# Four layers with mixtures of experts on one core: indirect transfers of layer 1's second list and of layer 2 in groups of four, each behind the last landing

## The chip, the cores and the metric

The kernel runs on one core of a Trainium2 chip. The metric is device time in microseconds (us), lower is better. Before the change the median of three runs is 2391.09 us (2387.86 to 2400.4). A core has a matrix engine (TensorE, PE in the profile), two engines for elementwise work (VectorE, DVE; ScalarE, ACT), a general engine that issues the indirect transfers here (GpSimd, POOL), and an engine that issues ordinary transfers (SyncE, SP). They run side by side, each through its own list of instructions in order, and wait for each other by semaphores.

## The reference

The input is 4 sequences of 1024 tokens with 128 features, float32. Eight sublayers follow, each of the form "normalise (x + f(x))":

```
x = norm(x + L0_attn(x))   gated scan over time        x = norm(x + L0_ffn(x))  a quantised linear layer
x = norm(x + L1_attn(x))   complex diagonal recurrence x = norm(x + L1_ffn(x))  16 experts, top 4, and a shared one
x = norm(x + L2_attn(x))   causal softmax, 16 heads    x = norm(x + L2_ffn(x))  8 low-rank experts, top 2
x = norm(x + L3_attn(x))   Toeplitz mix, 8 heads       x = norm(x + L3_ffn(x))  32 experts, top 4, and a shared one
```

In the three mixtures a token's result is a weighted sum over its few chosen experts. The reference applies every expert to every token and weights by zero where it was not chosen:

```python
combine = (one_hot(topk_idx, E) * tw[..., None]).sum(1)
h = einsum('td,edf->etf', x, gate_w);  u = einsum('td,edf->etf', x, up_w)
y = einsum('etf,efd->etd', silu(h) * u, down_w)
routed = einsum('etd,te->td', y, combine)
```

## The kernel before

The kernel computes an expert only for the tokens that chose it. The 4096 tokens are 32 tiles of 128, held on the chip in `self.x`. For each mixture and each part of the tokens, a routing step (`l1_route`, `l2_route`, `l3_route`, which end in `positions`) works out, for every token and each of its k choices, a row number in a list that is sorted by expert. The row numbers stand in a tile named `pos` plus the list's name. Lists are tensors in device memory.

A list is filled by `spread` (L1313): for each tile of 128 tokens and each of the k choices one indirect transfer writes the tile's 128 rows of 512 bytes to the 128 positions. The experts then read the list four tiles at a time through `gathered` (L1328, an SP transfer `xg<-...` that waits for all transfers of the spread), compute, and write their rows to a second list. `collect` (L1381) brings the results back: per tile k indirect transfers into a tile `yt`, and then k DVE operations at L1392 that multiply by the routing weight and add to `x`. All indirect transfers, in both directions, are issued by `indirect` on POOL (L1301). Names in the profile follow: `l1rr<-x,posl1r` is a scatter of layer 1's list r, `yt<-l1yr,posl1r` a gather of its results.

Layer 1 has two lists: a (the first half of the sequences, 64 transfers each way) and r (the second half, 64). Layer 2 has three, from two halves of attention: a2 (32 transfers each way), m2 and n2 (16 each). Layer 3 has a (64), b and c (32 each).

The order of the program is written by Python generators. Each step of a generator emits some instructions and yields their planned time in us. `mix(main, side)` (L238) runs the main generator and, after each of its steps, as many side steps as fit in its planned time; the side's instructions thus fall between those of the main one in each engine's list. `chain` puts generators one behind the other, `abreast` beside each other, `served` starts another one when a condition holds, and `press` runs a side alone until a condition holds. `self.now` is the sum of planned time. `moved_by` is the planned end of the indirect transfers so far; each adds 1.26 us. `collect` emits a tile's additions once `now` has passed its planned end by 4 us, or waits for that when the `yt` buffers (five for l1r, eight for l2a) are all in use.

The stages that matter here, from `all` (L1895), with the time at which each ran in the profiled execution:

- about 620 to 890 us: `l2_attn(0)`, attention of layer 2 for the first half, with the routing and the spread of l1r beside it.
- 890 to 1058 us: the experts of l1r and its shared expert, with the routing and the spread of l2a (`routed(a2)`) beside them.
- 1058 to 1207 us: `l2_experts(a2)`, with `l1_close(r)` beside it, which collects l1r's results, normalises, saves x (`xsave`) and transposes for the next attention.
- 1207 to 1603 us: `l2_attn(1)`, with `rows_in(a2)` (the collection of l2a's results), then `onward(a)`, layer 3's mix, routing and spread for part a, and `routed(m2)` when half of the rows are ready, `routed(n2)` when all are.
- 1603 to 1864 us: `l2_experts(m2)` and `l2_experts(n2)`, with what is left of that side.
- from about 1890 us: layer 3's shared expert and experts, part by part, with spreads and collections between them.

On POOL, the indirect transfers are kept in their order by two order-only dependencies on the last transfers (`self.moved`). They do not wait for each other's landing. Transfers of one spread are declared independent (`apart`), because they write different rows. POOL also reads, ahead of a rarely taken branch, how many tiles a list uses (`rest_of`, L1354).

Of the kernel before, what the change touches and what calls it, by code (L numbers as in the profile page):

```python
# [21 lines left out]
B, L, D = 4, 1024, 128  # L22
# [18 lines left out]
E1, F1, NG1, TKG1, K1 = 16, 128, 4, 2, 4  # L41
# [33 lines left out]
class Kernel:  # L75
    def __init__(self, ctx, tc, ins, out, cols, consts, rows):
        self.tc, self.nc, self.ins, self.out = tc, tc.nc, ins, out
        self.count = itertools.count()
        nc = self.nc
        self.const = self.pool(ctx, "const")  # L80
        self.small = self.pool(ctx, "small", 3)
        self.routes = self.pool(ctx, "routes")
        self.side = self.pool(ctx, "side", 2, space=PSUM)
        dram = self.pool(ctx, "dram", space=DRAM)

        self.cols_t = self.load(self.const, ins["cols"])
        self.cst_t = self.load(self.const, ins["consts"])
        self.x = self.tile(self.const, [P, NT, D], "x")
        self.xT = self.tile(self.const, [P, NT * P], "xT")
        nrow = ins["rows"].shape[1]  # L90
        self.rows_t = self.tile(self.const, [P, nrow], "rows")
        nc.gpsimd.dma_start(out=self.rows_t, in_=ins["rows"].to_broadcast([P, nrow]))
        self.col = {k: self.cols_t[:, a:b] for k, (a, b) in cols.items()}
        self.cst = {k: self.cst_t[:, a:b] for k, (a, b) in consts.items()}
        self.row = {k: self.rows_t[:, a:b] for k, (a, b) in rows.items()}
        self.ident = self.cst["ident"]
        self.eps = self.tile(self.const, [P, 1], "eps")
        nc.vector.memset(self.eps, LN_EPS)
        self.halfpi = self.tile(self.const, [P, 1], "halfpi")
        nc.vector.memset(self.halfpi, math.pi / 2)  # L100
        self.ones = self.tile(self.const, [P, E3], "ones")
        nc.vector.memset(self.ones, 1.0)
        self.rnd = self.tile(self.const, [P, 1], "rnd")
        nc.vector.memset(self.rnd, RND)
        self.zero = self.tile(self.const, [P, D], "zero")
        nc.gpsimd.memset(self.zero, 0.0)
        self.flag = self.tile(self.const, [1, 1], "flag", I32)
        self.hm = self.tile(self.const, [P, 4], "hmg")

        self.first, self.rest = Part("a", 0, 2), (Part("b", 2, 1), Part("c", 3, 1))  # L110
        self.parts = (self.first, *self.rest)
        self.by_rows = (
            Part("a", 0, 2, range(B), 0), Part("m", 2, 2, (0, 1), NT // 2), Part("n", 2, 2, (2, 3), 3 * NT // 4)
        )

        self.rows_done = 0

        self.listed = set()

        self.traced, self.latest = nc.cur_bb.bb.instructions, {}  # L120
        self.now = self.moved_by = 0.0
        self.moved = []

        self.lists, self.route = {}, {}
        self.both = (self.first, Part("r", 2, 2))
        for lay, ne, k in (("l1", E1, K1), ("l2", E2, K2), ("l3", E3, K3)):
            for pt in {"l1": self.both, "l2": self.by_rows, "l3": self.parts}[lay]:
                tl = -(-((pt.nt * P * k + (P - 1) * ne) // P) // 4) * 4
                self.lists[lay, pt.name] = (
                    self.tile(dram, [tl * P, D], f"{lay}r{pt.name}"), self.tile(dram, [tl * P, D], f"{lay}y{pt.name}"), tl  # L130
                )
        self.wall2 = self.tile(dram, [P, E2 * 3 * F2], "wall2")
        self.xsave = self.tile(dram, [P, NT, D], "xsave")

        self.ksave = self.tile(dram, [P, B, BLK], "ksave")
        self.vsave = self.tile(dram, [P, B, 4, (NH + 1) * VW], "vsave")
# [1162 lines left out]
    def indirect(self, apart=(), **kw):  # L1299

        ins = self.nc.gpsimd.indirect_dma_start(**kw)  # L1301

        for o in apart:
            self.tc.declare_no_dep(ins.ins, o.ins.name, reason="rows differ")
        behind = mybir.DependencyInfo(mybir.DependencyClass.NoSync, mybir.DependencyReason.DATA)
        mine = [o.ins.name for o in apart]
        for o in [o for o in self.moved if o not in mine][-2:]:
            self.tc.add_manual_dep(ins.ins, o, behind, reason="queued behind")
        self.moved = self.moved[-130:] + [ins.ins.name]
        self.moved_by = max(self.moved_by, self.now) + 1.26  # L1310
        return ins

    def spread(self, lay, part, k):  # L1313

        pos, _, _, done, _ = self.route[lay + part.name]
        rows = self.lists[lay, part.name][0]
        for t in range(part.nt):
            for i in range(k):
                ins = self.indirect(
                    apart=done,  # L1320
                    out=rows, out_offset=bass.IndirectOffsetOnAxis(ap=pos[:, t, i : i + 1], axis=0),
                    in_=self.x[:, part.order[t], :], in_offset=None,
                )
                done.append(ins)
            yield (1.26 * k,)
        self.listed.add(lay + part.name)

    def gathered(self, pool, rows, g, done, want):  # L1328
# [52 lines left out]
    def collect(self, lay, part, k, yp, first=0, nt=None, which=None):  # L1381

        nc = self.nc
        pos, wk = self.route[lay + part.name][:2]
        assert f"made {lay}{part.name}" in self.listed
        ys = self.lists[lay, part.name][1]
        late = []

        def add():
            t, yt, _ = late.pop(0)  # L1390
            for i in range(k):
                nc.vector.scalar_tensor_tensor(  # L1392
                    self.x[:, part.order[t], :], yt[:, i, :], wk[:, t, i : i + 1], self.x[:, part.order[t], :],
                    ALU.mult, ALU.add,
                )

        for t in which or range(first, first + (nt or part.nt)):
            yt = self.tile(yp, [P, k, D], "yt")
            for i in range(k):
                self.indirect(  # L1400
                    out=yt[:, i, :], out_offset=None, in_=ys,
                    in_offset=bass.IndirectOffsetOnAxis(ap=pos[:, t, i : i + 1], axis=0),
                )

            late.append((t, yt, self.moved_by + 4.0))
            if len(late) == yp.bufs:
                while late[0][2] > self.now:
                    yield (1.0,)
                add()
            yield (1.26 * k,)  # L1410
        while late:
            while late[0][2] > self.now:
                yield (1.0,)
            add()
            yield (0.36 * k,)
# [479 lines left out]
    def all(self):  # L1895
        a, rest = self.first, self.rest
        b, c = rest
        r = self.both[1]
        a2, m2, n2 = self.by_rows
        with ExitStack() as ctx:  # L1900
            lgp = self.pool(ctx, "l2lg")
            self.l2_lg = self.tile(lgp, [P, NT, E2], "lg")
            with ExitStack() as early:
# [13 lines left out]
                with ExitStack() as c2:  # L1917
                    wall = self.l1_wall(c2)
                    yp = self.pool(c2, "l1ya", 5, right=True)
# [2 lines left out]
                    self.run(self.mix(self.abreast(self.l2_weights(), side), self.l1_close(a, yp)))  # L1922
            with ExitStack() as c2:
                wall = self.l1_wall(c2)
                self.run(self.mix(self.l2_attn(0), self.chain(self.l1_route(r), self.spread("l1", r, K1))))
                wall2, loads = self.l2_wall(c2, True)
                yp = self.pool(c2, "l1yr", 5, right=True)
                self.run(self.mix(self.chain(self.l1_experts(r, wall), self.l1_shared(r)), self.chain(loads, self.routed(a2))))
                self.run(self.mix(self.l2_experts(a2, wall2), self.l1_close(r, yp)))
            listed = lambda name: lambda: name in self.listed  # L1930
            on = self.served(
                self.chain(self.rows_in(a2), self.onward(a, True)),
                (lambda: self.rows_done >= B + 2, self.routed(m2)),
                (lambda: self.rows_done == 2 * B, self.routed(n2)),
            )
            self.run(self.mix(self.l2_attn(1), on, drain=False))
            with ExitStack() as c3:
                with ExitStack() as c2:
                    wall = self.l2_wall(c2)
# [7 lines left out]
                yp = self.pool(c3, "l3y", 8)  # L1947
# [23 lines left out]
        with self.tc.If(bad > 0):  # L1971
            with ExitStack() as ctx:
# [9 lines left out]
                for p in self.parts:  # L1982
                    self.run(self.onward(p))
                    with ExitStack() as c2:
                        sw, wall = self.l3_wall(c2)
# [167 lines left out]
```

## Time and profile before

| what | value |
|---|---|
| median of three runs | 2391.09 us |
| profiled execution, its own time | 2410.17 us |
| span in the profile, mean granted TensorE clock | 2408.4 us, 0.828 |
| PE busy | 1599.0 us (66%), 9017 matmuls |
| DVE busy | 1262.4 us (52%) |
| ACT busy | 822.5 us (34%) |
| POOL busy | 720.1 us (30%) |
| indirect transfers, queue q0 | 20704 packets, 42.86 MB, 5.8% of 16 DMA engines |
| l1rr<-x: 64 transfers | 699.1 to 779.9 us, median 958 ns |
| l2ra<-x: 32 transfers | 951.5 to 991.7 us, median 958 ns |
| yt<-l1yr: 64 transfers | 1021.3 to 1180.3 us, median 945 ns |
| yt<-l2ya: 32 transfers | 1210.1 to 1289.8 us, median 944 ns |
| l2rm<-x and l2rn<-x: 16 transfers each | from 1483.9 and from 1647.8 us, median 958 ns |

The time of a transfer in the table is how long POOL is busy with it; between two that follow each other POOL shows 0.30 us more. Busy time counts only work: register, branch, semaphore and transfer-issuing instructions of the other engines are not in it. Idle time of an instruction is put down to a releaser, the instruction of another engine whose signal came last before it started. "Issue" is idle time in which the engine waited for nothing that the profile shows; "remote" is a wait for a signal whose sender the profile can't place as late.

### The profile page before, as it was taken

The numbers are of one execution on the slowest core, as the hardware profiler recorded it, in microseconds if no ns is written. First come the engines' busy times: TensorE is split into PE (matmuls) and PEld (weight loads), VectorE is DVE, ScalarE is ACT, GpSimd is POOL, SyncE is SP. The second block draws the span as 40 slices with busy tenths as digits, with TensorE's granted clock in tenths as the row PEclk, the third lists the DMA queues.
The fourth block names the chain that finished last, engine by engine and source line by source line (L and its number), as shares of the span: only waits on it lengthen the run. The fifth ranks groups of instructions, "written<-read, shape, count | busy, mean of one in ns | idle before, by whom it ended". The sixth has DMA issues, their size and how long they took to land. (4 is left out here: it accounts for less than half of the span.)

```text
span 2408.4 us, 27028 instructions
## 1 busy us (share of the span) xinstructions
PE 1599.0 (66%) x9017; PEld 956.7 (40%) x9017; DVE 1262.4 (52%) x3630; ACT 822.5 (34%) x1179; POOL 720.1 (30%) x681
## 2 busy tenths in 40 slices
PE   7625776975661778487969797887735798357160
PEld 3214334843320347344623232344423486155160
DVE  8857894655570655224535674573602265237133
ACT  6701671422230433122336554632101164233030
POOL 1031483135227001325132002002272200735725
PEclk9866887988785889688979998988877899678575
DMA  9930002334101015212130000031411131222232
GB/s 309 288 112 0 21 34 93 115 115 157 62 30 50 15 54 185 81 42 76 40 101 21 1 1 18 1 119 36 160 71 32 42 113 49 78 81 59 90 88 68
DMA packets 215529, 187.10 MB, mean 78 GB/s; under 512 B 16528, under 2 KB 194064, under 8 KB 214864
## 3 DMA queue, kind: packets, MB, share of 16 engines
q1 hardware_dynamic: 194672, 142.29, 18.7%
q0 software_dynamic: 20704, 42.86, 5.8%
q8 instruction: 84, 1.38, 0.2%
q14 instruction: 69, 0.57, 0.1%
HBM read 88.49 MB, written 96.60 MB: 77 GB/s over the span
## 5 line engine op out<-in xcount | busy, mean ns | idle before, releaser
L1055 ACT ACTIVATE pr<-sc 128x1024 f32<-128x1024 f32 x288 | 279.5, 1021 | 319.3 <-PE sc L157 186.3
L157 PE MATMUL gu<-ld,xgT 128*128 x640 | 176.9, 423 | 75.3 <-ACT xgT L167 57.4
L157 PE MATMUL sc<-qm,kT 32*128 32x512 f32 (+3 forms) x1536 | 200.0, 555 | 14.2 <-ACT pr L1055 7.4
L157 PE MATMUL s<-pr,va 128*32 128x512 f32 (+3 forms) x1536 | 174.0, 520 | 45.9 <-issue 25.9
L1755 DVE TENSOR_TENSOR hg<-sg,gu 128x256 f32<-128x256 f32 x160 | 65.7, 417 | 210.7 <-ACT sg L1754 194.9
L157 PEld LDWEIGHTS gu<-ld,xgT 128*128 128x128 f32 x640 | 127.9, 211 | 104.6 <-ACT xgT L167 60.7
L165 PE MATMUL tp<-ld,hg 128*128 128x128 f32 x624 | 103.5, 288 | 95.2 <-DVE hT L169 44.2
L157 PE MATMUL gu<-wall,xgT 128*128 x304 | 155.0, 636 | 2.7 <-ACT xgT L167 2.0
L169 DVE COPY hT<-tp 128x512 f32<-128x512 f32 x118 | 80.9, 686 | 140.5 <-remote 65.5
L1061 DVE TENSOR_TENSOR pr<-pr,ld 128x512 f32<-128x512 f32 (+1 forms) x160 | 92.2, 580 | 101.0 <-ACT pr L1055 98.5
L165 PE MATMUL tp<-ld,xg 128*128 128x128 f32 x396 | 67.7, 300 | 112.4 <-DMA xg<-l3rc 50.3
L165 PEld LDWEIGHTS tp<-ld,hg 128*128 128x128 f32 x624 | 81.1, 148 | 147.6 <-issue 62.7
L167 ACT COPY xgT<-tp 128x512 f32<-128x512 f32 x99 | 57.8, 585 | 236.9 <-PE tp L165 130.4
L157 PEld LDWEIGHTS sc<-qm,kT 32*128 32x128 f32 x1536 | 85.1, 195 | 116.4 <-issue 76.5
L1507 ACT ACTIVATE sg<-gu 128x512 f32<-128x512 f32 x76 | 45.2, 597 | 215.3 <-PE gu L157 104.9
L1754 ACT ACTIVATE sg<-gu 128x256 f32<-128x256 f32 x160 | 60.9, 384 | 151.5 <-PE gu L157 78.2
L1301 POOL DMA_INDIRECT l1ra<-x,posl1a x64 | 93.0, 1454 | 59.0 <-DVE posl1a L1276 39.8
L157 PEld LDWEIGHTS s<-pr,va 128*32 128x32 f32 x1536 | 38.5, 111 | 153.7 <-issue 106.3
L1301 POOL DMA_INDIRECT yt<-l1yr,posl1r x64 | 60.8, 950 | 127.9 <-DVE x L1392 80.1
L165 PEld LDWEIGHTS tp<-ld,xg 128*128 128x128 f32 x396 | 50.9, 155 | 118.9 <-issue 74.5
L1509 DVE TENSOR_TENSOR hg<-sg,gu 128x512 f32<-128x512 f32 x76 | 51.8, 681 | 80.5 <-ACT sg L1507 57.9
L1301 POOL DMA_INDIRECT l1rr<-x,posl1r x64 | 61.5, 961 | 100.0 <-DVE posl1r L1276 80.8
(440 smaller groups left out, 3471.0 us busy)
## 6 DMA issues: line engine op xcount, KB each, us to landing
wall<-wall SPq DMA_DIRECT2D x16, 768.0 KB
l3ra<-zero SPq DMA_DIRECT2D x1, 6144.0 KB
ld<-in_l_w SPq DMA_DIRECT2D x2, 3072.0 KB
wall<-we SPq DMA_DIRECT2D x24, 256.0 KB
ld<-in_l_w SPq DMA_DIRECT2D x1, 6144.0 KB
l1ra<-zero SPq DMA_DIRECT2D x1, 5120.0 KB
l1rr<-zero SPq DMA_DIRECT2D x1, 5120.0 KB
xg<-l3ra SPq DMA_DIRECT2D x20, 256.0 KB
```

Source lines behind the costliest of these rows:

```text
L157: return self.nc.tensor.matmul(out, lhsT, rhs, start=start, stop=stop)
L165: nc.tensor.transpose(pt[:, k * P : (k + 1) * P], s, self.ident)
L167: nc.scalar.copy(dst, pt[:, : n * P])
L169: nc.vector.tensor_copy(dst, pt[:, : n * P])
L1055: nc.scalar.activation(pr, sc[h], AF.Exp)
L1061: nc.vector.tensor_tensor(d, d, cst["tril"].unsqueeze(1).unsqueeze(1).to_broadcast([P, 2, n, P]), ALU.mult)
L1301: ins = self.nc.gpsimd.indirect_dma_start(**kw)
L1507: nc.scalar.activation(sg, gu[:, 0, :], AF.Silu)
L1509: nc.vector.tensor_tensor(h, sg, gu[:, 1, :], ALU.mult)
L1754: nc.scalar.activation(sg, pg[:, :, 0, :], AF.Silu)
L1755: nc.vector.tensor_tensor(h[:, 2 * c : 2 * c + 2, :], sg, pg[:, :, 1, :], ALU.mult)
```

## The change

Indirect transfers get an optional spacing, three values: `every`, `back` and `step`. While a spacing is set, `before` counts the transfers of the run; the transfer with number n (from 0), where n is a multiple of `every` and not 0, waits for the landing of transfer n minus `back`. With 4, 1, 1.75 the fifth transfer waits until the fourth has landed, the ninth until the eighth, and so on. The planned time of one transfer, in `moved_by` and in the steps that `spread` and `collect` yield, is then 1.75 instead of 1.26 us. A generator is wrapped by `spaced`, which sets the spacing before each of its steps and clears it after.

Wrapped are the spread of l1r (64 transfers), `routed(a2)` (32), `l1_close(r)` (64), `rows_in(a2)` (32), `routed(m2)` and `routed(n2)` (16 each): 224 transfers, 56 groups. Not wrapped are layer 1's list a in both directions, the collections of m2 and n2, and everything of layer 3. Numbers of instructions and their data stay as they are; the planned times shift where the side's instructions fall between those of the main generator.

```diff
@@ in indirect
         ins = self.nc.gpsimd.indirect_dma_start(**kw)
 
+        landed = self.before(ins)
         for o in apart:
-            self.tc.declare_no_dep(ins.ins, o.ins.name, reason="rows differ")
+            if o is not landed:
+                self.tc.declare_no_dep(ins.ins, o.ins.name, reason="rows differ")
...
-        self.moved_by = max(self.moved_by, self.now) + 1.26
+        self.moved_by = max(self.moved_by, self.now) + self.step
         return ins
+
+    @property
+    def step(self):
+        return self.spacing[2] if self.spacing else 1.26
+
+    def before(self, ins):
+
+        if not self.spacing:
+            self.landing = []
+            return None
+        every, back, _ = self.spacing
+        n = len(self.landing)
+        self.landing.append(ins)
+        if n < back or n % every:
+            return None
+        o = self.landing[n - back]
+        self.tc.add_manual_dep(
+            ins.ins, o.ins.name,
+            mybir.DependencyInfo(mybir.DependencyClass.Sync, mybir.DependencyReason.DATA),
+            reason="behind its landing",
+        )
+        return o
+
+    def spaced(self, gen, *spacing):
+
+        while True:
+            self.spacing = spacing
+            got = next(gen, None)
+            self.spacing = None
+            if got is None:
+                return
+            yield got
@@ in spread, and the same in collect
-            yield (1.26 * k,)
+            yield (self.step * k,)
@@ in all
-                self.run(self.mix(self.l2_attn(0), self.chain(self.l1_route(r), self.spread("l1", r, K1))))
+                self.run(self.mix(self.l2_attn(0), self.chain(self.l1_route(r), self.spaced(self.spread("l1", r, K1), 4, 1, 1.75))))
...
-                self.run(self.mix(self.chain(self.l1_experts(r, wall), self.l1_shared(r)), self.chain(loads, self.routed(a2))))
-                self.run(self.mix(self.l2_experts(a2, wall2), self.l1_close(r, yp)))
+                self.run(self.mix(self.chain(self.l1_experts(r, wall), self.l1_shared(r)), self.chain(loads, self.spaced(self.routed(a2), 4, 1, 1.75))))
+                self.run(self.mix(self.l2_experts(a2, wall2), self.spaced(self.l1_close(r, yp), 4, 1, 1.75)))
...
-                self.chain(self.rows_in(a2), self.onward(a, True)),
-                (lambda: self.rows_done >= B + 2, self.routed(m2)),
-                (lambda: self.rows_done == 2 * B, self.routed(n2)),
+                self.chain(self.spaced(self.rows_in(a2), 4, 1, 1.75), self.onward(a, True)),
+                (lambda: self.rows_done >= B + 2, self.spaced(self.routed(m2), 4, 1, 1.75)),
+                (lambda: self.rows_done == 2 * B, self.spaced(self.routed(n2), 4, 1, 1.75)),
```

More of the change, by code (lines that the diff above doesn't have):

```diff
@@ L1309, in indirect @@
         self.moved = self.moved[-130:] + [ins.ins.name]
-        self.moved_by = max(self.moved_by, self.now) + 1.26
+        self.moved_by = max(self.moved_by, self.now) + self.step
         return ins
+    @property
[3 more added lines that the diff above has]
+        if not self.spacing:
+            self.landing = []
+            return None
[15 more added lines that the diff above has]
+            got = next(gen, None)
+            self.spacing = None
+            if got is None:
+                return
+            yield got
     def spread(self, lay, part, k):
@@ L1409, in collect @@
                 add()
-            yield (1.26 * k,)
+            yield (self.step * k,)
         while late:
```

## The prediction

> **What bounds the kernel now.** I read the page first, by slices. The rows are TensorE (PE), ScalarE (ACT) and GpSimd (POOL) in 40 slices of 60.2 us, each digit the busy share in tenths.
>
> ```profile
> PE   7625776975661778487969797887735798357160
> ACT  6701671422230433122336554632101164233030
> POOL 1031483135227001325132002002272200735725
> ```
>
> No engine is full throughout: PE is busy 66% of the span. Slices 12 and 13 (662 to 783 us) hold PE 6, then 1, ACT 3 then 0, where POOL goes from 2 to 7. When POOL issues its indirect transfers, the others stop. The chain that ended last covers only the final 55 us, so it says nothing of this place.
>
> The second view is busy time by window: columns are length, then PE, its weight load, VectorE (DVE), ACT and POOL busy with instruction counts, granted clock, DMA share, GB/s.
>
> ```profile
> 640.00:699.00 59.00, 48.06 (x386) 22.68 (x386) 41.22 (x168) 29.33 (x31) 0.00 (x0) 0.88 0.04 15
> 700.00:780.00 80.00, 18.47 (x96) 6.63 (x94) 13.22 (x47) 3.98 (x4) 60.65 (x64) 0.57 0.13 52
> 950.00:1000.00 50.00, 17.47 (x97) 14.97 (x96) 9.77 (x39) 5.89 (x14) 30.62 (x32) 0.70 0.24 81
> 1000.00:1020.00 20.00, 17.44 (x109) 15.91 (x107) 8.63 (x16) 6.58 (x14) 0.00 (x0) 0.89 0.32 101
> ...
> 267.00:361.00 94.00, 70.29 (x318) 31.19 (x311) 88.23 (x112) 65.42 (x72) 78.85 (x50) 0.85 0.09 34
> ```
>
> The attention of layer 2's first half does 386 matmuls in 59 us; while l1rr's 64 scatters go out it does 96 in 80 us. The experts of l1r do 97 in 50 us beside l2ra's 32 scatters and 109 in the 20 us after. DMA stands at 0.13 and 0.24, so bandwidth isn't it. The last row is layer 1's first list: POOL is as dense, but the others run on.
>
> The third view is the waits in 700 to 790 us: who waited for what, total, times, longest.
>
> ```profile
> ACT pr L1055 <- remote: 74.7, 3, 72.5
> DVE t L169 <- remote: 59.7, 1, 59.7
> PE s L157 <- issue: 24.7, 12, 2.4
> ```
>
> "Remote" is a signal of another engine that is not seen to be late: ACT's next exponential waits 72.5 us though its scores were done. In the timeline PE meanwhile issues one matmul of 0.37 us every 2.8 us:
>
> ```profile
> 753.43 0.37 PE L157 MATMUL s<-pr,va 128*32 128x128 f32 x1 [2.43 <-issue]
> 756.23 0.37 PE L157 MATMUL s<-pr,va 128*32 128x128 f32 x1 [2.43 <-issue]
> ```
>
> ACT moves again at 786.3, 6.5 us after the last transfer. So the signals between engines stand while transfers run back to back. I can't name the mechanism, only its dose. Durations by source line (min/median/max ns), and a lone group of four inside attention, by window:
>
> ```profile
> L1301 POOL DMA_INDIRECT l1ra<-x,posl1a x64: 954/974/3007, 267.2 to 378.5; - x64
> L1301 POOL DMA_INDIRECT l1rr<-x,posl1r x64: 954/958/1184, 699.1 to 778.9; - x64
> ...
> 1268.00:1275.00 7.00, 6.76 (x53) 2.22 (x48) 1.26 (x5) 5.15 (x6) 3.78 (x4) 1.00 0.15 39
> ```
>
> l1ra spreads 64 transfers over 111.3 us (1.77 us each) with no wait for a remote signal; only its last 15, at 1.26 us, bring a long wait (ACT 13.8 us). l1rr issues every 1.26 us: freeze from about the tenth. Four at 1.25 us and then a pause: PE busy 6.76 of 7 us. The change makes every long burst a row of such fours.
>
> **The change part by part.**
>
> *The period of a group.* Three steps of 1.26 us, then the landing of the fourth. In the packet and signal records a scatter lands a median 2.05 us after its start, a gather 2.23 to 2.33. Then POOL must start: l2ra's positions ended at 951.26 and its first transfer began at 951.54, 0.28 us. So 3.78 + 2.05 + 0.28 = 6.1 us per scatter group against 5.05, and 6.3 per gather group: 1.53 and 1.58 us a transfer. Over 224 transfers (64 l1rr, 64 l1yr, 32 l2ra, 32 l2ya, 16 l2rm, 16 l2rn; 56 groups) POOL needs some 65 us more. The planned step of 1.75 is above what I expect, so planned ends come late rather than early.
>
> *Two rules weighed.* The Trainium skill, "DMA: Bandwidth & Descriptors", § Rules for kernel authors, says to wait late on a DMA's semaphore so that its fixed cost is overlapped; § Anatomy of one DMA puts a transfer at 2.0 us plus bytes over 436 GB/s, 2.15 us for the 65,536 bytes here. That speaks against the change: were every group's landing exposed, 56 x 2.15 = 120 us more, 2511. The rows say otherwise: POOL isn't what these stages wait for, and the added part of a landing is about 1.1 us. I go by the rows. The second: "SBUF — State Buffer", § Who interferes with whom, says only DVE and GpSimd can block each other, by a lock on a shared port. l1ra's row fits (POOL stretched to 3007 ns beside a dense DVE). But in l1rr's burst POOL keeps 958 ns and it's ACT and PE that stand, so the lock isn't the freeze. By that rule the pauses would give back next to nothing (rival B); by the rows nearly all.
>
> *What goes.* Work done in each frozen window, priced at the matmul rate of the window beside it:
> - l1rr: 96 matmuls at 386/59 = 6.54 a us are 14.7 us; the window took 80: 65 us.
> - l2ra: 97 at 109/20 = 5.45 are 17.8 of 50: 32 us.
> - l1yr (bursts of 20, 8, 16, 8, 12 from 1021 to 1180): remote waits of DVE of 11.3 at 1031 and 12.2 and 7.3 later are 31; PE still works through part: 25 us.
> - l2ya: 1226 to 1237 holds 25 matmuls where the next 30 us run 6.73 a us: 3.7 of 11, 7 us. The earlier part is under loads at 293 GB/s, not counted.
> - l2rm: 101 at 242/43 = 5.63 are 17.9 of 23: 5 us.
> - l2rn: 13 in 1658 to 1671 at 138/29 = 4.76 are 2.7 of 13: 10 us.
>
> Sum 144 us. By waits alone (72.5 for l1rr, 31 for l1yr, 14 for l2rm) it would be up to 170.
>
> *What is added on the path.* Residual freeze: the lone four cost nothing visible, bursts of eight 2 to 5 us; between 0 and 28 us over 56 groups (half a us each), I take 12, nearer the four. A wait sits at the head of POOL's queue: behind it are only transfers and the reads of the used-tile counts ahead of a branch; no wait names those reads, so I give them nothing. Who waits for lists: xg of l1rr is first needed at 889.8, 110 us after its end; its spread will take 98 us instead of 81 while attention ends 65 earlier, leaving about 28 us of cover (if gone, each us late counts whole). l2ra is needed at 1058.7, 67 us after its end; 32 x 0.27 = 9 us longer, 32 earlier: covered. l1yr's collections start behind l2ra in the queue and need five yt buffers free, so their adds (0.35 us each on L1392) follow them; in the built order the last adds, the norm and the transposes of l1_close now fall behind l2_experts(a2), bare before l2_attn(1): from 0 to 30 us, I take 10. l2ya's plan is 32 x 0.49 = 16 us longer, and what onward(a) does with layer 3 moves later against l2_attn(1) and l2_experts(m2): 0 to 20, I take 5, since l3ra's spread lies in l2_experts(n2), whose own freeze (unspaced, 1758 to 1806) stays. SP's gathers and xsave stores only follow these.
>
> *Sum, against the profiled execution:* 2410.17 - 144 + 12 + 10 + 5 = 2293. The runs' median is 19 us under the profiled time, so 2274. (That the two differ by 19 only also says that the freezes aren't made by profiling.)
>
> **Rivals.**
> - A: freeze cured, gain as summed. For it: the lone four, l1ra, and l3ra's transfers with gaps at 1738 to 1750, where PE keeps 17.1 of 20 us. Against: no row shows fours repeated with only a 1 us pause. Own range: best 170 with no residue and 5 of lateness, 2226; worst 110 with 28 and 30, 2339.
> - B: slower. The pause between groups is too short for the hand-offs, the backlog carries over from group to group, and the freezes last the whole longer bursts. Place: l1rr and l2ra. Price: 224 x 0.29 = 65 plus 15 of lateness: 2471. It decides when under 38% of the 144 comes back: f x 144 = (1 - f) x 65 + 15. For it: ACT stayed frozen 6.5 us past the last transfer, longer than any pause.
> - C: freezes cured, gain given back. The late l1_close and onward(a) leave l3ra's list late, so that the drain ahead of layer 3 is bare: 30 to 60 us more, 2305 to 2385 with A's poorer end: 2345. For it: the shifted order; against: nothing waited for POOL long in 1210 to 1712.
> - D: nothing measurable; the freeze has another cause than transfer density, and the longer bursts hide: 2391. Against: every back-to-back burst over eight in these stages freezes.
>
> **How the numbers follow.** A 0.66, B 0.15, C 0.14, D 0.05. Likeliest 2274; A's own range 2226 to 2339. The range reaches over C's part to 2385 and a little under A, leaving out B and some of D: 2220 to 2385. Within 0.5% of the median (12 us) is about what a measurement can't tell from no change. Faster: A, and C: 0.80. Same: D 0.05. Slower: B 0.15.
>
> **What would show it.** Right: in l1rr's window ACT's remote wait of 72.5 is gone, PE runs near 6 matmuls a us, the spread takes 95 to 112 us; l2ra's 50; xg of l1rr comes near 825. The freeze beside l3ra stays. Wrong: remote waits of tens of us inside spaced bursts (B); a gap of over 20 us on PE ahead of l2_attn(1) or layer 3 (C); landings well over 2.3 us, which make groups longer than 7 us.

## The result, and the profile after

The changed kernel takes 2379.16 us (median of 12 runs, 2372.48 to 2390.3), the kernel before in the same comparison 2391.01 us: a ratio of 0.9946, 95% interval 0.9922 to 0.997. It is 12 us faster, where 117 us were forecast (2274 us, range 2220 to 2385). The profiled executions show 2410.17 us before and 2374.06 us after; 2410.17 us lies above all twelve timed runs before (at most 2403.27), so 24 of these 36 us are not the change's. I read differences of stages from the profiles and their worth from the timed ratios.

The page of the changed kernel by slices (PE, ACT, POOL, 59.3 us a slice):

```profile
PE   7725776975661688488798788977843798367170
ACT  6700571422230343122265554732210164233030
POOL 1031384145227000434221002002164200735725
```

The hole of slices 12 and 13 (counted from 1) is still there: PE 6 and 1, ACT 3 and 0, beside POOL 2 and 7. The same by window (columns as in the prediction); the first row is l1rr's spread, the second l2ra's, the third the first twenty gathers of l1yr:

```profile
692.00:773.00 81.00, 18.66 (x96) 6.70 (x96) 14.61 (x51) 3.99 (x4) 61.33 (x64) 0.56 0.13 51
945.00:995.00 50.00, 17.55 (x92) 14.96 (x91) 9.26 (x27) 5.89 (x13) 30.80 (x32) 0.69 0.26 85
1014.00:1046.00 32.00, 29.83 (x113) 16.82 (x114) 9.64 (x14) 6.56 (x11) 19.00 (x20) 0.92 0.24 69
```

l1rr still holds 96 matmuls in 81 us and l2ra 92 in 50: nothing has changed beside the scatters. Beside the gathers it has: 113 matmuls in 32 us, with PE busy 29.8 of them, where 56 were done in 29 us before:

```profile
1021.00:1050.00 29.00, 18.72 (x56) 10.24 (x56) 3.59 (x6) 3.15 (x6) 18.97 (x20) 0.80 0.22 58
```

The waits in 690 to 800 us of the changed kernel tell the same of l1rr (total, times, longest):

```profile
ACT pr L1057 <- remote: 71.5, 2, 69.7
DVE t L171 <- remote: 62.4, 1, 62.4
```

And so does POOL's timeline, here l1rr's ninth to eleventh transfer and then l1yr's fourth to sixth:

```profile
702.85 0.96 POOL L1303 DMA_INDIRECT l1rr<-x,posl1r  x1 [0.30 <-issue]
704.12 0.96 POOL L1303 DMA_INDIRECT l1rr<-x,posl1r  x1 [0.30 <-issue]
705.38 0.96 POOL L1303 DMA_INDIRECT l1rr<-x,posl1r  x1 [0.30 <-issue]
...
1017.87 0.95 POOL L1303 DMA_INDIRECT yt<-l1yr,posl1r  x1 [0.30 <-issue]
1021.05 0.95 POOL L1303 DMA_INDIRECT yt<-l1yr,posl1r  x1 [2.24 <-PE py L159]
1022.30 0.95 POOL L1303 DMA_INDIRECT yt<-l1yr,posl1r  x1 [0.30 <-issue]
```

The gathers go out in fours with a gap of some 2 us. The scatters show no such gap: 64 in 81 us, as before. The built program says why. These are l1rr's first nine transfers on POOL with their waits; the numbered DMASW semaphores are handed out in turn, and a transfer waits for the last user of its own:

```
164 L1303 DMACopy l1rr_91<-x_73,posl1r_4630 10240x128 [waits DMASW2_49,DVE_49]
165 L1303 DMACopy l1rr_91<-x_73,posl1r_4630 10240x128 [waits DMASW3_49]
166 L1303 DMACopy l1rr_91<-x_73,posl1r_4630 10240x128 [waits DMASW4_49]
167 L1303 DMACopy l1rr_91<-x_73,posl1r_4630 10240x128 [waits DMASW5_49]
168 L1303 DMACopy l1rr_91<-x_73,posl1r_4630 10240x128 [waits DMASW6_49]
169 L1303 DMACopy l1rr_91<-x_73,posl1r_4630 10240x128 [waits DMASW7_49]
170 L1303 DMACopy l1rr_91<-x_73,posl1r_4630 10240x128 [waits DMASW0_49]
171 L1303 DMACopy l1rr_91<-x_73,posl1r_4630 10240x128 [waits DMASW1_49]
172 L1303 DMACopy l1rr_91<-x_73,posl1r_4630 10240x128 [waits DMASW5_49,DMASW2_49]
```

The transfer that waits for the fourth's landing (DMASW5) is issued ninth, not fifth. It is the list's fifth transfer. Transfers of one spread are declared independent and have no order among themselves (`apart`), so the scheduler put four others ahead of the one that had to wait: three of its own group and one of the next. The ninth starts 6.3 us after the fourth (702.85 against 696.52), and a scatter lands in some 2.2 us (the median of before_again, shown further down). So the fourth had landed long before, and the wait cost nothing and did nothing. Gathers write into `yt` and are tied to the last two transfers in order, so there the wait holds back all that follow.

### The profile page after: what moved, and what is told of

The parts are those of the page before. It is cut to its first block, busy times and chain, and to the rows that moved or that the text cites. A ratio compares the mean times of both kernels' runs of the same rounds, so it can differ in the third digit from the quotient of the medians.

```text
span 2371.9 us, 27047 instructions
## 1 busy us (share of the span) xinstructions
PE 1592.9 (67%) x9017; PEld 955.2 (40%) x9017; DVE 1263.3 (53%) x3630; ACT 824.5 (35%) x1180; POOL 719.2 (30%) x681
## 5 line engine op out<-in xcount | busy, mean ns | idle before, releaser
L159 PE MATMUL gu<-ld,xgT 128*128 x640 | 179.2, 427 | 83.5 <-issue 39.4
L167 PE MATMUL s<-ld,x 128*128 128x128 f32 x128 | 30.7, 368 | 99.6 <-DVE x L211 74.5
L1303 POOL DMA_INDIRECT l3ra<-x,posl3a x64 | 61.7, 964 | 108.6 <-DVE posl3a L1278 83.8
```

The lines of the kernel that those rows point to most:

```text
L159: return self.nc.tensor.matmul(out, lhsT, rhs, start=start, stop=stop)
L167: nc.tensor.transpose(pt[:, k * P : (k + 1) * P], s, self.ident)
```

## The experiments

The record gives the chip of each experiment a number. On chips 1, 10 and 7 the kernel before takes 2407, 2394 and 2398 us, on chip 0 it takes 2053 us. I call the first three the slow chips and chip 0 the quick chip. For the result no number is given; with 2391 us it belongs to the slow ones. Every ratio is to the kernel before on the same chip in the same series of runs. Where one variant ran on two of the slow chips, its two ratios agree within 0.0005. All variants are edits of the changed kernel.

**Make the groups real.** Every transfer of a later group waits for the last landing of the group before it. On every other engine the order is the changed kernel's.

```diff
-        if n < back or n % every:
+        if n < every:
             return None
-        o = self.landing[n - back]
+        o = self.landing[n - n % every - back]
```

> The changed kernel, but every scatter of a later group waits for the last landing of the group before it, so that none can be put ahead of the waiting one. In the changed kernel's trace the 128 spaced scatters still go out every 1.27 us. Theory F (freezes come from long runs of transfers, a pause of 1 us after four cures them): l1rr takes 95 to 105 us instead of 81, ACT's remote wait of 70 us in it goes, and the time falls by some 100 us against the changed kernel (65 + 32 + 5 + 10 of the prediction, less 10): 2265 to 2300. Rival G (the pause is too short for scatters): freezes stay and last longer, 128 x 0.27 = 35 us more: 2390 to 2420. Rival H (freezes go, but the gain is lost at a later wait, for l3ra's list): 2330 to 2360.

Slow chip 1: 2263.69 us, ratio 0.9394 (0.937 to 0.9418). Theory F holds, at the lower edge of its range. l1rr's window and POOL's waits in it, in this variant:

```profile
702.00:804.00 102.00, 78.09 (x663) 36.69 (x667) 66.33 (x180) 40.70 (x42) 63.76 (x64) 0.91 0.15 58
...
POOL l1rr L1303 <- DMA l1rr<-x,posl1r: 21.6, 14, 1.6
```

Beside the same 64 scatters, over 102 us, PE does 663 matmuls, 6.5 a us, the rate of the attention without them. POOL now waits for landings, 1.6 us at most.

**Drop the scatters' waits.**

```diff
-        landed = self.before(ins)
+        landed = self.before(ins) if kw["out_offset"] is None else None
```

> The changed kernel without the landing waits of the scatters; planned times and the order on every engine as in the changed kernel. If the scatters' waits are without effect there, as the trace suggests, the time is the changed kernel's, 2370 to 2390. If they do cost or bring something, over 10 us off that.

Slow chip 1: 2390.6 us, ratio 0.9934 (0.9914 to 0.9953), which overlaps the changed kernel's 0.9946. The scatters' waits in the changed kernel do nothing that the time shows.

**Keep the planned step, drop all waits** (`before` always returns None). Run twice.

> The changed kernel's planned step of 1.75 us, with no landing wait at all. If the gathers' waits make the gain: 2385 to 2400, and the remote waits of 11 and 12 us beside l1yr's gathers are back. If the gain comes from the later place of the additions and of what follows: 2370 to 2385.

> plan_only again: the planned 1.75 us without waits. On the chip without freezes: if the plan is what costs there, ratio 1.015 to 1.025, with l3ra's spread some 40 us later behind l2rn's than before; if the waits do, 0.997 to 1.005. On the chip with freezes: 1.003 to 1.007, as measured.

Slow chips 1 and 10: 2419.84 us, 1.0051 (1.0031 to 1.007), and 2407.6 us, 1.0055 (1.0038 to 1.0072). The first lies above both ranges that were expected: the step itself costs 13 us against the kernel before (2406.7 and 2394.36 us). The gathers' waits bring what lies between 1.0051 and 0.9934, 28 us of 2391. What is left is 16 us in gathers_only and 12 in the result, the change's gain. (Without the gathers' waits the additions of l1yr's results also change places: VectorE's order differs at 34 places from the changed kernel's, TensorE's at 3.)

**Groups of eight** (8, 1, 1.75 with the real grouping).

> As true_fours, in groups of eight. Theory F with a freeze that begins after about ten transfers: each group of eight loses 2 to 5 us at its end, 28 groups some 60 to 100 us if all of it is on the path, so that the time lies between: 2300 to 2350. If eight are short enough: as true_fours or a little less (28 fewer pauses). If the pause cures nothing: 2385 to 2400.

Slow chip 1: 2338.57 us, ratio 0.9705 (0.9682 to 0.9729), inside what a freeze from about the tenth transfer gives. In l1rr's window ACT still waits 22.8 us for remote signals, in three pieces of at most 9.2 us. Eight are too many, but half of the cure.

**Pause without a landing, twos, a smaller planned step, more of the kernel.** All four ran on the quick chip.

```diff
+            for _ in range(3):
+                m = self.nc.gpsimd.memset(self.idle, 0.0)   # in order after the group, ahead of the next
```

> As true_fours, but no transfer waits for a landing: after every four GpSimd fills a small tile three times (about 1 us) before the next. If the pause in the issue is what cures: l1rr takes 95 to 110 us, no remote wait of over 10 us in it, and the time is true_fours' within 20 us (ratio to before 0.935 to 0.95). If it is the landing, or GpSimd's idle sequencer, that cures: freezes as before and 35 us or more of longer spreads, ratio 0.99 to 1.02.

> As true_fours, in groups of two. A group takes 1.26 + 2.05 + 0.3 = 3.6 us, 1.8 us a transfer, l1rr 115 us. If four still leave some of the freeze: another 5 to 15 us less, ratio 0.933 to 0.938. If four are short enough: the longer spreads are hidden or cost up to 20 us, ratio 0.938 to 0.948.

> As true_fours, with a planned step of 1.55 us, near the measured 1.6. If the planned 1.75 costs what plan_only suggests (its 13 us over before): up to 10 us less, ratio 0.935 to 0.939. If not: the same within 5 us.

> As true_fours, and the same for layer 1's first list in both directions, for what onward(a) spreads (l3ra) and for the collection of l2m: 208 more transfers. Their freezes in true_fours (idle of PE, DVE and ACT at once beside l3ra and l2ym, 1599 to 1702 us, some 75 us of it over 2 us long) should go: 40 to 80 us less than true_fours, ratio 0.905 to 0.925. If layer 3's start waits for the end of l3ra's longer spread instead: less than 25 us, ratio 0.93 to 0.94.

Quick chip, kernel before 2053.26 us: ratios 1.0181 (1.0133 to 1.0228), 1.0365 (1.0315 to 1.0416), 1.0105 (1.0063 to 1.0148) and 1.052 (1.0479 to 1.0561). All four expectations were made for a slow chip and failed here: everything is slower, the smaller step least, twos and more of the kernel most. Four repeats on the quick chip show why:

> The kernel before, unchanged, for a second profile of it. In the last call the kernel before took 2053 us, on another chip than the 2407 us of the call ahead of it. If this runs on the chip of 2053 us: no freeze in l1rr (PE over 5 matmuls a us in it, no remote wait over 10 us), the span about 2050. If on the other: as in the profile before, about 2400 us with a remote wait of some 70 us in l1rr.

> The changed kernel again. On the chip without freezes its waits and later plan can only cost: ratio to before 1.005 to 1.02. On the one with freezes: 0.99 to 0.997, as measured.

> true_fours again. On the chip without freezes: ratio 1.005 to 1.025 (fours_155 had 1.01). On the one with freezes: 0.937 to 0.942, as measured.

> pause_only again. On the chip with freezes this tells a pause in the issue from a landing: 0.935 to 0.95 if the pause cures, 0.99 to 1.02 if the landing does. On the one without freezes: 1.01 to 1.025, as measured.

The kernel before, profiled on the quick chip: span 2049.1 us. l1rr's and l2ra's windows and l1rr's transfers:

```profile
675.00:760.00 85.00, 70.47 (x623) 34.08 (x615) 61.16 (x165) 37.15 (x39) 65.00 (x64) 0.93 0.18 68
853.00:893.00 40.00, 35.63 (x215) 29.59 (x214) 17.93 (x41) 13.73 (x29) 30.38 (x32) 0.91 0.48 154
...
L1301 POOL DMA_INDIRECT l1rr<-x,posl1r x64: 954/958/1460, 675.8 to 759.9; - x64
```

The same program, transfers of the same 958 ns, the last packet of one ending 1.86 us after its start where it was 1.85 (medians, from the packets in both traces), and no freeze: 623 matmuls beside l1rr where the slow chip does 96. On this chip the change costs 1.0215 (1.0191 to 1.024), real fours 1.0195 (1.0164 to 1.0226), the pause 1.0193 (1.0158 to 1.0229). The change and real fours take the same time, 2097 and 2096 us, and differ in the scatters' waits, which are without effect in the first and real in the second. So on the quick chip the scatters' waits in fours cost nothing that shows.

Where do the change's 44 us on this chip go? The answers for layer 3's first list and for l2n's, first of the kernel before, then of the changed kernel, both on the quick chip (first and last start at the end of a row):

```profile
L1332 SPq DMA_DIRECT2D xg<-l2rn x5: 359/360/476, 1491.6 to 1518.0; - x5
L1301 POOL DMA_INDIRECT l3ra<-x,posl3a x64: 952/958/1336, 1496.2 to 1583.8; - x64
L1332 SPq DMA_DIRECT2D xg<-l3ra x20: 359/360/508, 1611.4 to 1682.1; - x20
```

```profile
L1368 SPq DMA_DIRECT2D xg<-l2rn x5: 359/359/430, 1505.7 to 1546.6; - x5
L1303 POOL DMA_INDIRECT l3ra<-x,posl3a x64: 952/958/1160, 1544.8 to 1630.9; - x64
L1368 SPq DMA_DIRECT2D xg<-l3ra x20: 359/360/517, 1659.9 to 1729.9; - x20
```

From the first tile of l2rn to the first scatter of l3ra it's 4.6 us before and 39.1 after, and layer 3's first tile comes 119.8 us after l2rn's before and 154.2 after. 34 of the 44 us arise here. The distance is the plan's: with steps of 1.75 us, the side chain reaches layer 3's routing later against the main one. The distance of 4.6 to 39 us is in the built order, for it is nearly the same on the slow chips: 4.7 us before, 39.5 in the changed kernel and in plan_again, which has no wait at all. With a step of 1.55 us (fours_155) it's 18.7 us, and the loss is 21 us rather than 44. The quick chip's loss from the step alone was not measured.

**Waits alone, with the plan of before** (4, 1, 1.26 and the real grouping: on every engine the order of the kernel before), and the same with fills in place of landings, and with more of the kernel.

> true_fours with the planned step of before, 1.26 us: every engine has exactly the order of the kernel before, and the landing waits of all 224 transfers are the one difference. On the chip without freezes: if the plan is what costs there, ratio 0.997 to 1.005; if the waits do, 1.01 to 1.025. On the chip with freezes: 0.93 to 0.94 (0.9394 less plan_only's 0.5%).

> As fours_126, with three small fills on GpSimd (about 1 us) in place of each landing wait. On the chip with freezes: 0.93 to 0.945 if the pause in the issue cures, 0.99 to 1.03 if the landing does. On the one without: 0.997 to 1.008.

> As fours_126, and in true groups of four too: layer 1's first list both ways, l3ra and the collection of l2m. On the chip with freezes: what is left of them beside these goes, 40 to 80 us less than fours_126, ratio 0.90 to 0.92. On the one without: the longer spread of l3ra is waited for, ratio 1.005 to 1.03.

> fours_126 again. On the chip with freezes as measured, 0.92 to 0.926. On the one without: 0.997 to 1.005 if the planned step made the 2%, 1.01 to 1.025 if the waits did.

Slow chip 10: 0.9231 (0.92 to 0.9262), again on slow chip 7 0.9226 (0.9174 to 0.9279); with fills 0.9263 (0.923 to 0.9295); with layer 1's first list, l3ra and l2ym too 0.9123 (0.9093 to 0.9153). The waits and the fills do better than was expected (0.93 to 0.94 and 0.93 to 0.945): with the cure in place the planned step costs 1.6% (0.9394 against 0.9231), three times what it costs alone; l3ra's first scatter is 4.6 us behind l2rn's first tile here, 39.4 in true_fours.

The fills show that no transfer has to wait for a landing. POOL's timeline around the first group and l1rr's window in pause_126:

```profile
698.98 0.99 POOL L1306 DMA_INDIRECT l1rr<-x,posl1r  x1 [0.30 <-issue]
699.96 1.08 POOL L1341 MEMSET idle<- 128x256 f32 x3
701.20 1.20 POOL L1306 DMA_INDIRECT l1rr<-x,posl1r  x1 [0.16 <-issue]
...
695.00:793.00 98.00, 77.37 (x695) 36.41 (x687) 67.79 (x179) 41.46 (x43) 79.23 (x110) 0.94 0.16 60
```

POOL is busy through the pause and waits for no landing, and PE does 695 matmuls in 98 us. About 1.2 us without a transfer after every four is enough. One thing this can't tell: the next group starts 2.2 us after the fourth transfer did (701.20 against 698.98), which is about when that one has landed. A shorter pause wasn't tried, so a rest between issues and having no transfer under way are not told apart.

In more_126 the stretch from l3ra's first scatter to layer 3's first tile is 144 us (1531 to 1675), against 200 us in fours_126 (1523 to 1723), for the same 528 or 529 matmuls. Of these 56 us, 26 are left in the time (2182.86 against 2208.63 us), fewer than the 40 to 80 expected: l3ra's spread starts 8 us later, and what follows layer 3's first tile takes 15 us longer.

**The largest term alone**: real fours in l1rr, nothing else, plan of before.

> The kernel before, with true groups of four in l1rr alone; order on every engine as before. On the chip with freezes the prediction's term for l1rr, 65 us less (55 to 75): ratio 0.969 to 0.977. If what is won there is lost again at a later wait: over 0.985. On the chip without: 0.998 to 1.004.

Slow chip 7: 2326.44 us, ratio 0.9696 (0.9643 to 0.9748), 73 us of 2391 with an interval of 60 to 85. No later loss shows within that interval. The two profiles of the kernel before give the same price without an edit: from l1rr's first transfer to the first tile read from its list it takes 190.7 us on the slow chip (699.1 to 889.8) and 117.9 on the quick one (675.8 to 793.7), 73 us less.

## Why the prediction was wrong

**The reading of what bounds the kernel was right** for the slow chips. Long runs of indirect transfers stop the hand-offs between the other engines, and four with a pause don't: true_fours, pause_126 and l1rr_only show it by the edit alone. "The chain that ended last says nothing of this place" also held.

**The step that failed** is "The change makes every long burst a row of such fours". It does so for the 96 gathers and not for the 128 scatters: l1rr still held 96 matmuls in 81 us, against 663 in 102 once its groups were real, and the 112 us that were counted for the scatters stayed. The reason stood in the code (`apart` frees the transfers of a spread from any order) and in the built order (the second wait on the ninth transfer, not the fifth). By the names of tiles all 64 transfers are alike; only the semaphores tell them apart. None of the rivals was that the change doesn't do what it says; D, "nothing measurable", had a different cause.

With the four scatter terms struck (65 + 32 + 5 + 10), the prediction's sum is 25 + 7 = 32 us gained, less 5 of residue (96 of 224 transfers of the 12), 10 for l1_close and 5 for onward(a): 12 us faster, what was measured. Its two halves hold too: 27 us brought by the gathers (32 less 5), where 28 were measured, and 15 lost to later work, where the planned step costs 13. The split of the second half doesn't:

- *The gathers' 32 us*, 27 less residue: 28 measured (plan_only to gathers_only), residue and lateness of waiting included.
- *The scatters' 112 us*: 129 where they are really grouped (gathers_only to true_fours, 0.9934 to 0.9394). l1rr's 65: 73 measured.
- *l1_close, 10 us*: not measured apart.
- *onward(a), 0 to 20 us, 5 taken*: mis-sized. l3ra's spread starts 35 us later behind l2rn. In the two profiles of the result, layer 3's first tile comes 207 us after l2rn's before and 222 after, 15 us; on the quick chip it's 34. I had argued that l3ra lies inside l2_experts(n2) anyway, and had not asked how far behind its start. Rival C named this place, and its mechanism is real, but it is not what made the forecast fail.
- *The period of a group, 6.1 us*: l1rr takes 102.6 us in true_fours, 6.4 a group. The landing in it, 2.05 us for a scatter, was read from incomplete records: counted in the trace before, 146 of the 1024 landing signals of l1rr's 64 transfers are there (16 each), so mostly not the last one. Where they are complete, the profile gives a median of 2.2 us for a scatter and 2.5 for a gather; first the kernel before on the slow chip, without a landing, then on the quick chip:

```profile
l1rr<-x,posl1r POOLq DMA_INDIRECT x64
l1rr<-x,posl1r POOLq DMA_INDIRECT x64, 2.2
yt<-l1yr,posl1r POOLq DMA_INDIRECT x64, 2.5
```

- *110 us of slack ahead of xg of l1rr*: enough; it comes at 824.6 us in true_fours, as forecast ("near 825").
- *Rival C's range, 2305 to 2385*: 30 to 60 us on A's poorer end of 2339 would reach 2369 to 2399, so its upper end was set too low.

**Rival B** (the pause is too short) fell: the pause of about 1.2 us suffices. Whether a longer one does better on a slow chip wasn't tried. **The rule that speaks against the change** (the Trainium skill, "DMA: Bandwidth & Descriptors", § Rules for kernel authors, wait late), at its face an estimated 2511 us, did not hold here: the waits of all 224 transfers together, with the plan of before, come out at 0.9231 on a slow chip. On the quick chip, where nothing is to be cured, groups of two go the rule's way (1.0365 against 1.0195 for fours, with the same planned step), and the scatters' waits in fours cost nothing that shows.

What stays open is why three chips freeze and one doesn't. The length of a transfer (958 ns) and the time to its last packet (1.85 and 1.86 us) are alike. The quick chip's granted clock is higher (0.871 against 0.828), but in the frozen windows engines wait rather than run slowly. One difference stands in the traces themselves. Of the 1024 landing signals of l1rr's transfers, the trace of the kernel before holds 146 on the slow chip and 1011 on the quick one, and that of true_fours 577 on the slow one. So it is in every trace: of the 10240 landing signals of all indirect transfers, those from slow chips hold 3395 to 5862, those from the quick chip practically all. Whether the freeze holds back the signals, or the recording of signals is part of what freezes the engines, no run here tells: every timed run on record carries a granted clock, so each was recorded in some measure. The prediction's remark that the freezes aren't made by profiling is therefore not shown. What all the waits together cost on the quick chip with the plan of before wasn't measured either.

## What to carry to other kernels

A wait added to one of several instructions that have no order among themselves delays that one only; the scheduler fills its place with the others. See on which instruction of the built order the wait stands, and whether what it waits for can still be unfinished there, before pricing what it does; names alone don't show it. And when a change moves planned times, look for the first list or load that moves behind its consumer's stage: here a step of 1.75 instead of 1.26 us put layer 3's spread 35 us later and took back 13 of the 28 us that the gathers' pauses brought.

## What the runs showed of the hardware

The same program takes 2394 to 2407 us on three chips and 2053 us on another, and most of the difference is in one behaviour: on the three, long runs of indirect transfers issued every 1.26 us all but stop PE, DVE and ACT (96 matmuls in 80 us beside l1rr), on the other they don't (623 in 85 us). Of the 359 us between the spans of the two profiles of the kernel before, the stretches of four lists hold 234: 73 from l1rr's first transfer to the first tile read from it, 88 likewise for l3ra, 29 from l2ra's first transfer to l1yr's, and 44 from l1yr's first transfer to its last. On the slow chips, a pause of about 1.2 us after four ends the freeze in l1rr, a pause after eight brings half as much, and it makes no difference beyond the intervals whether GpSimd waits or works in the pause. The fastest version there, real groups of four with the plan of before in more of the kernel, takes 2182.86 us, 0.9123 of the kernel before and well under the changed kernel; on the quick chip its counterpart with the larger step was 5.2% slower than before. A schedule tuned on one chip isn't tuned for the other.
